# A mixture-of-experts kernel: the shared expert's gate and up as one-pass products of split operands, with most rows kept in HBM

## The chip, the cores and the metric

The kernel runs on one core of a Trainium2 chip. Its time is the device time of one execution, in microseconds (us). The trace comes from one profiled execution of the same program. Engines are named as in the profile: PE multiplies matrices, DVE and ACT do elementwise work, POOL and SP mostly issue DMAs; PEld is PE's loading of weights.

## The reference

The input x is [128, 64, 512]: 128 sequences of 64 steps with 512 features, all in float32. Two layers follow one another, each added to its input:

```python
x = x + ternary_ffn(gru(cond_2048, x))        # a scan over 64 steps
h = conv_causal(x, cond_2048) + b
x = x + moe(h) + shared(h)

# ternary_ffn: scale = mean(|W|); W3 = clip(round(W / scale), -1, 1) * scale; y = x @ W3.T + bias
# shared(h)  = silu(h @ sw_gate) * (h @ sw_up) @ sw_down       # 512 -> 704 -> 512, for all 8192 rows
# moe(h): softmax over 64 experts, the best 6 of them; each expert takes its first 64 rows,
#         silu(h @ w_gate) * (h @ w_up) @ w_down (512 -> 352 -> 512), weighted and summed
```

The sums of the 704 hidden features are what the change recomputes in another form; "gate" and "up" are the two products h @ sw_gate and h @ sw_up, "down" is the third.

## The kernel before

**Three stages.** The GRU goes through its 64 steps one after another (to about 1215 us). The causal convolution follows, as products with banded matrices (to about 1276 us). The last stage, to the end, holds router, shared expert and routed experts. It runs in iterations i = 0 to 15 of four steps each (NB = 4, so 512 rows). Iterations 0 to 7 are interleaved with the routing of all 16 blocks of rows, iterations 8 to 15 with the 64 routed experts, two at a time.

**Two ways to multiply float32.** A plain float32 product takes PE two instructions. A value can instead be split in two: the high part (`masked`, the low 12 bits cut off), and the rest. Three planes are then made, named h, l and s (the scaled mix of both), and a product becomes three one-pass products in type fp32r, hh, ll and ss, in two banks a and b, joined when the banks are emptied (`a * WHOLE + b`). The GRU is computed so, and the down product of iterations 1 to 7 (lines 1124 and 1137, planes `dparts` of the weights and `aparts` of the hidden values). A split costs DVE three operations and ACT one or two for each piece of 128 x 512 (lines 350, 1203, 1205).

**Seven products for eight.** The gate and up of all iterations go another way: `shared` treats the four steps and the four blocks of features as a 2 x 2 matrix of blocks and computes seven products of 256 columns in place of eight, in plain float32 (`winograd`, line 830, driven by class `Block`, lines 843 to 877). It needs sums and differences of the weights (`prepare_shared`, lines 790 to 793, tiles `st1`, `st2`, `st4`), made on DVE in iteration 0, and of the rows (the tile `space`). The 704 features are five chunks of 128 and a rest of 64, which line 1006 multiplies plainly. Iterations from 8 on use the same scheme for the down product too.

**Where rows are.** The convolution leaves its rows in two SBUF tiles, `hid0` and `hid1`, 32 steps each. All 64 steps are also stored to a table in HBM, `tab`, from which the routed experts gather (`put_rows`, line 1342), 40 of them issued on SP at 1281 us. `hid1`'s room becomes free when its rows are there; the planes of the down weights are put into it (`split_down`, line 1193 on). Blocks 8 to 15 come back from the table two at a time to be routed (`fetch_rows`, line 1374). After iteration 7 they come back as rows already turned, from a table `xts` (`load_xrows`, line 1431).

**Routing.** `route` turns a block's rows (line 1238), multiplies with the gate (1262), makes the softmax and picks six of 64 experts on DVE. It counts, in the tile `cum`, how many rows of each expert came up to each step. After iteration 7 `count_slots` makes the slots from this: a product psb (line 1515), then carry, `far` (1545), its absolute value on ACT (1555), a comparison (1556), and the products `found` (1572).

**What sets the order.** The code is written as generators: `for n, _ in enumerate(shared(i))` advances the shared expert by one group of products and takes pieces of `routing` and of `split_down` between. The order that is written is kept mostly; a scheduler may move an instruction ahead of others that do not need it, on the same engine, unless `tc.issue_after` ties it to another. Each engine then works its list strictly in order. Tiles in a pool wait for whoever used their room before.

**The steps of the GRU that matter here.** In step t, four transposes turn the state (`pst`, line 422), DVE and ACT split it into hh, hl and hs (lines 350, 356, 357, 436), and PE multiplies these with `whh` (line 339). In steps 2 and 3 DVE also converts the last of the GRU's weights (`convert`, lines 350, 367, 369), and step 3 has the sums for the ternary weights (`ternary`, line 463).

## Time and profile before

| what | value |
|---|---|
| median of 3 runs (lowest to highest) | 2431.18 us (2430.2 to 2432.18) |
| the profiled execution | 2432.05 us |
| its span, first to last instruction | 2430.1 us |
| granted clock of PE, mean | 0.999 |
| PE busy / PEld / DVE / ACT / POOL | 2416.7 / 1875.9 / 1588.1 / 502.7 / 447.7 us |
| DMA moved | 330.74 MB, 136 GB/s over the span |
| starts of iterations 0 to 8 (line 1006) | 1281.35, 1342.98, 1400.59, 1458.00, 1515.40, 1572.81, 1630.21, 1687.61, 1741.86 |

In the lines of the page and of the timelines, a group is named by its line, engine and operation, then output tile <- input tiles, the shape, and x followed by the number of instructions. In a timeline the first column is the start, the second the time from the start of the group's first instruction to the end of its last; in square brackets stands how long the engine was idle before it, and which instruction ended that. In a table by stretches each line has the stretch, its length, the busy time of PE, PEld, DVE, ACT and POOL, then the granted clock of PE, the mean share of the 16 DMA engines that was busy, and GB/s.

### The profile page before, as it was taken

The page shows a single profiled execution, that of the slowest core. Times are in us where ns is not written, and L with a number is a line of the kernel's source. Part 1 is how long each engine was busy: PE and PEld are TensorE (multiplying, and loading weights), DVE is VectorE, ACT ScalarE, POOL GpSimd, SP SyncE. Part 2 cuts the span into 40 slices and gives each one's busy share as a digit, 9 for nine tenths or more (in the row PEclk, how much of TensorE's full clock was granted, in tenths as well). Part 3 has the DMA queues.
Part 4 walks back from the last instruction along what each step waited for, and adds up shares of the span by engine and source line. Part 5 has one row for each costly group of instructions (what it writes and reads, how often), then busy time and mean ns, then how long its engine had stood idle before and what let it go on. Part 6 is the DMA issues. An engine that isn't in the chain of part 4 may idle for free.

```text
span 2430.1 us, 32183 instructions
## 1 busy us (share of the span) xinstructions
PE 2416.7 (99%) x12221; PEld 1875.9 (77%) x12221; DVE 1588.1 (65%) x3146; ACT 502.7 (21%) x920; POOL 447.7 (18%) x470
## 2 busy tenths in 40 slices
PE   9999999999999999999999999999999999999999
PEld 5788888888888888888896787888876666676667
DVE  8877777777777777777687767777753333343344
ACT  5211111111111111111123333333311111111111
POOL 1222221112112211221221000000012222222220
PEclk9999999999999999999999999999999999999999
DMA  5244443333222223222498223343459999899961
GB/s 189 76 85 85 81 77 63 61 68 67 58 56 61 58 53 58 60 57 44 110 344 299 42 43 72 102 114 91 143 147 291 290 297 308 265 320 312 281 176 40
DMA packets 469098, 330.74 MB, mean 136 GB/s; under 512 B 317136, under 2 KB 384720, under 8 KB 466768
## 3 DMA queue, kind: packets, MB, share of 16 engines
q1 hardware_dynamic: 439904, 254.47, 36.9%
q0 software_dynamic: 28896, 73.95, 13.4%
q8 instruction: 97, 1.59, 0.3%
q14 instruction: 57, 0.47, 0.1%
q10 hardware_dynamic: 144, 0.26, 0.0%
HBM read 241.83 MB, written 92.03 MB: 137 GB/s over the span
## 4 chain that ended last, share of the span: by engine, by line
PE 98%; DVE 1%; DMA 0%; ACT 0%; issue 0%; DVEq 0%; ACTq 0%
PE psa L339 9%; PE psw L339 9%; PE psx L339 9%; PE psz L830 7%; PE psw L830 7%; PE psx L830 7%; PE psb L339 5%; PE psz L339 5%; PE psy L339 5%; PE psf L339 5%; PE y L830 4%; PE py L1694 3%; PE pg L1668 3%; PE pu L1668 3%; PE y L1006 2%; PE psc L194 2%
## 5 line engine op out<-in xcount | busy, mean ns | idle before, releaser
L1678 DVE SCALAR_TENSOR_TENSOR a<-a,rw,pu 128x352 f32<-128x352 f32 x32 | 18.6, 580 | 213.0 <-PE pu L1668 198.8
L357 DVE SCALAR_TENSOR_TENSOR xs<-xl,xcut 128x512 fp32r<-128x512 f32 x63 | 103.6, 1644 | 65.6 <-POOL xl L356 65.6
L1214 POOL DMA_DIRECT2D out_dram<-hid x60 | 53.3, 1079 | 447.4 <-DVE hid L1150 368.0
L830 PE MATMUL psx<-hid,sw 128*128 128x256 f32 x512 | 132.3, 381 | 0.4 <-ACT g L870 0.4
L350 DVE TENSOR_SCALAR hcut<-pst 128x512 int32<-128x512 int32 x63 | 43.5, 691 | 130.1 <-PE pst L422 128.4
L491 ACT ACTIVATE rz<-rz 128x512 f32<-128x512 f32 x64 | 40.5, 633 | 335.8 <-DVE rz L490 334.8
L356 POOL TENSOR_TENSOR xl<-xp,xcut 128x512 fp32r<-128x512 f32 x60 | 83.1, 1386 | 145.7 <-PE psa L339 132.8
L830 PEld LDWEIGHTS psx<-hid,sw 128*128 128x128 f32 x512 | 94.3, 190 | 15.7 <-issue 2.9
L436 ACT CAST hh<-hcut 128x512 fp32r<-128x512 f32 x61 | 37.9, 621 | 325.0 <-DVE hcut L350 325.0
L272 POOL DMA_DIRECT2D q<-in_x_dram x36 | 19.3, 537 | 411.0 <-DMA out_dram<-q 331.1
L1694 PE MATMUL py<-wd,aeT 128*64 128x512 f32 (+1 forms) x288 | 88.6, 595 | 0.0
L830 PE MATMUL psw<-hid,st 128*128 128x256 f32 x320 | 83.0, 382 | 0.0
L1668 PE MATMUL pg<-wg,hid 128*64 128x352 f32 x384 | 81.1, 459 | 0.0
L1668 PE MATMUL pu<-wu,hid 128*64 128x352 f32 x384 | 81.1, 459 | 0.0
L1705 POOL DMA_INDIRECT out_dram<-hid,idxp x32 | 46.2, 1444 | 177.3 <-DMA out_dram<-hid,idxo 89.1
L1705 POOL DMA_INDIRECT out_dram<-hid,idxo x32 | 45.4, 1420 | 175.4 <-DMA out_dram<-hid,idxp 161.6
L870 ACT ACTIVATE g<-psx 128x256 f32<-128x256 f32 x80 | 30.7, 383 | 215.8 <-DVE aT L877 101.8
L504 ACT ACTIVATE n<-n 128x512 f32<-128x512 f32 x64 | 40.5, 633 | 166.7 <-DVE n L503 166.7
L339 PE MATMUL psa<-wih1h,xh 128*128 128x512 f32 x252 | 74.2, 415 | 0.0
L830 PE MATMUL y<-hid,st 128*128 128x256 f32 x280 | 74.0, 381 | 0.0
L272 POOL DMA_DIRECT2D xn<-in_x_dram x28 | 15.0, 536 | 318.4 <-DMA out_dram<-xn 271.1
L830 PE MATMUL psz<-hid,st 128*128 128x256 f32 x280 | 72.4, 380 | 0.0
(456 smaller groups left out, 6229.8 us busy)
## 6 DMA issues: line engine op xcount, KB each, us to landing
wg<-in_w_gate_dram SPq DMA_DIRECT2D x48, 704.0 KB
wu<-in_w_up_dram SPq DMA_DIRECT2D x48, 704.0 KB
wd<-in_w_down_dram SPq DMA_DIRECT2D x48, 512.0 KB
xc<-x1c SPq DMA_DIRECT2D x32, 512.0 KB
xp<-in_xT_dram POOLq DMA_DIRECT2D x62, 256.0 KB
out_dram<-hid POOLq DMA_DIRECT2D x60, 256.0 KB
tab<-hid SPq DMA_DIRECT2D x56, 256.0 KB
hid<-in_w_gate_dram SPq DMA_DIRECT2D x16, 704.0 KB
```

What stands on the lines that cost most here:

```text
L194: i = nc.tensor.matmul(ps[rows, j].rearrange("p h (u t) -> p h u t", u=2), xcs[sl % NCB][:, rows, g * 4 + j], tzs[sl % NCB][:, :, :, g * 4 ...
L339: i = nc.tensor.matmul(ps, lhs[:, k, :], rhs[:, k, :], start=start and k == 0, stop=stop and k == KD - 1, skip_group_check=True,)
L350: return nc.vector.tensor_scalar(dst.bitcast(I32), src.bitcast(I32), LOW, None, ALU.bitwise_and)
L356: i = engine.tensor_sub(lo, full, cut)
L357: nc.vector.scalar_tensor_tensor(mix, lo.bitcast(F32), -SPLIT, cut, ALU.mult, ALU.add)
L491: nc.scalar.activation(r, r, AF.Sigmoid)
L830: i = nc.tensor.matmul(ps.rearrange("p (j b) -> p j b", b=P) if len(r.shape) == 3 else ps, lhs(k), r, start=(first and k == 0), stop=(k == ...
L1006: nc.tensor.matmul(gu.rearrange("p (j b) -> p j b", b=P), swr[:, k].rearrange("p w n -> p (w n)"), rows[:, k], start=(k == 0), stop=(k == ...
L1214: nc.gpsimd.dma_start(out=out_t[t], in_=rows_of(i)[:, t % NB], accum_op=ALU.add)
L1668: nc.tensor.matmul(acc[halves[j]], self.xeT[:, k, halves[j]], self.ws[j][which][:, k, :], start=(k == 0), stop=(k == KD - 1),)
L1694: nc.tensor.matmul(py[halves[j]], self.aeT[:n, c, halves[j]], self.ws[j][2][:n, c, :], start=(c == 0), stop=(c == len(ech) - 1),)
L1705: nc.gpsimd.indirect_dma_start(out=out, out_offset=bass.IndirectOffsetOnAxis(ap=(idxp[:CAP] if j == 0 else idxo)[:, q : q + 1], axis=0), i ...
```

## The change

**Iterations 1 to 7** compute gate and up with split operands: for each chunk and for each of gate and up, three parts of four one-pass products of 512 columns (120 instructions in all). The weights' planes are `gparts` (g0 to g4, one for each chunk), the rows' planes `xparts`, made by `split_x(i + 1)` while the down products of iteration i run. ACT copies bank b, DVE joins both and multiplies. Iteration 0 computes gate and up as plain float32 products of 512 columns (`shared_plain`, 40 products). Iterations 8 to 15 are as before.

**Rows.** To make room, `hid0` keeps 12 steps (blocks 0 to 2), and `hid1` has the other 52. All 52 are stored in iteration 0 on SP, then their room becomes the planes g1 to g4, `dparts`, the scratch tiles `cut` and `xparts`. Every block from the fourth on is fetched from HBM for its iteration, into a ring of three areas in `hid0`; blocks are routed in a new order, as they are there, and 8 to 15 in between. The count in `cum` is started anew at step 32, and joined by one addition in `count_slots`.

**Weights.** In iteration 0 the shared weights are loaded ahead of the stores. After iteration 7 all pools are closed, the shared weights are loaded again (gate and up, 2.5 MB, and down, 1.28 MB), and `prepare_shared` runs there: chunk 0 between the iterations, 1 to 4 in iteration 8. `split_down` moves to iteration 1 and loads its pieces again.

**GRU.** In step 3 the products `psb <- wih1s, xs` come behind the transposes; the second half of the conversion in step 2 comes behind hs of that step; the sums for the ternary weights come behind the cell of step 3.

```diff
 def shared_split(i):                       # new, iterations 1 to 7
+    gu = rest_product(rows_by_k(i))
+    masters = [ring[:, c % 3] for c in range(full)]
...
+    for c in range(full):
+        for which in range(2):
...
+            for n, ps in ((2, b), (0, a), (1, a)):
+                for k in range(KD):
+                    m = nc.tensor.matmul(
+                        ps,
+                        gparts[c][n][:, which, k],
+                        xparts[n][:, k],
+                        start=n != 1 and k == 0,
+                        stop=n != 0 and k == KD - 1,
...
+                if n == 2:
+                    nc.scalar.copy(v, b)
...
+            nc.vector.scalar_tensor_tensor(v, a, WHOLE, v, ALU.mult, ALU.add)
+            if which == 0:
+                nc.scalar.activation(g, g, AF.Silu)
+                if c == 0:
+                    rest_split(sg, gu, aTr)
+            else:
+                mul(v, v, g)
+            next(split, None)
+            yield
...
+        split = split_block(masters[c], c)
+    downs.append([*split][-1])
+    yield from down_split(i)

+def split_x(i):
+    rows = rows_by_k(i)
+    for k in range(KD):
...
+        masked(cut, rows[:, k])
+        nc.scalar.copy(xh, cut)
+        nc.vector.tensor_sub(xl, rows[:, k], cut)
+        nc.vector.scalar_tensor_tensor(
+            xs, xl.bitcast(F32), -SPLIT, cut, ALU.mult, ALU.add
+        )
+        yield

 if i == 0:
+    for n in range(NEAR, NI):
+        put_rows(n)
     later.close()
...
+    work = (
+        w
+        for ws in (split_gate_up(0), split_x(1), *map(split_gate_up, range(1, full)))
+        for w in ws
+    )
 if i == 1:
...
+    work = split_down()

 def count_slots():
+    nc.vector.tensor_tensor(
+        cum[:, TH:],
+        cum[:, TH:],
+        cum[:, TH - 1 : TH].to_broadcast([P, TH, NE]),
+        ALU.add,
+    )

+w1 = ctx.enter_context(tc.tile_pool(name="w1", **right))      # after iteration 7
...
+load_xrows(HALF)
+load_sw(w1)
+load_swd()
...
+prepare_shared(0)

-            products(b, xs, ws, start=True, stop=c == 2)         # GRU, step 3
+            with tc.issue_after(turns[-1].ins) if (t, c) == (3, 1) else nullcontext():
+                products(b, xs, ws, start=True, stop=c == 2)
...
+                        convert(raw_h[c], whh[c], cuts, range(KD // 2))
+                        with tc.issue_after(mixes[-1].ins):
+                            convert(raw_h[c], whh[c], cuts, range(KD // 2, KD))
```

## Prediction

> **What bounds the kernel now.** I read the busy table and the chain's shares first, to learn which engine a saved microsecond must come from.
>
> ```profile
> PE 2416.7 (99%) x12221; PEld 1875.9 (77%) x12221; DVE 1588.1 (65%) x3146; ACT 502.7 (21%) x920; POOL 447.7 (18%) x470
> ...
> PE 98%; DVE 1%; DMA 0%; ACT 0%; issue 0%; DVEq 0%; ACTq 0%
> ```
>
> PE is idle for 13.4 us of the 2430.1 us span, so the time is PE's work plus very little. Any PE work saved counts in full, any wait that the change puts in front of PE counts in full too, and there are no gaps in which a new wait could hide. Second, the table by stretches, for the stage that is changed:
>
> ```profile
> 1400.00:1500.00 100.00, 100.00 (x505) 80.41 (x504) 74.17 (x206) 36.06 (x70) 5.20 (x6) 1.00 0.25 57
> 1305.00:1310.00 5.00, 5.00 (x29) 4.39 (x28) 4.01 (x11) 0.60 (x2) 0.00 (x0) 1.00 1.04 396
> ```
>
> In a hundred microseconds of iterations 2 and 3, PE is busy for 100.0, DVE for 74 (fourth value), ACT for 36, and the granted clock is 1.00. Between 1305 and 1310 the DMA engines are full (share 1.04, 396 GB/s): those are the rows going to HBM. Third, PE's timeline, for the price of one product in each form:
>
> ```profile
> 1560.98 1.07 PE L1124 MATMUL psw<-dl,al 128*128 128x512 f32 x4
> 1561.89 1.07 PE L1124 MATMUL psz<-ds,as 128*128 128x512 f32 x4
> ...
> 1576.56 1.03 PE L830 MATMUL psx<-hid,sw0first 128*128 128x256 f32 x4
> 1577.43 1.03 PE L830 MATMUL y<-hid,st 128*128 128x256 f32 x4
> ...
> 1324.05 7.89 PE L1099 MATMUL y<-swd,aT 128*128 128x512 f32 x18
> 1331.87 1.13 PE L1109 MATMUL y<-swdr,aTr 64*128 64x512 f32 x4
> ```
>
> I take start to start. Four one-pass instructions of 512 columns take 0.907 us, 0.2268 each. A 7-product block's product of 256 columns is two instructions (x4 is two products): 0.865 / 2 = 0.4325. Plain fp32 of 512 columns: 18 instructions in 7.82 us, two to a product, 0.868.
>
> **Iterations 2 to 6: -15.3 us.** The old gate and up are 5 chunks x 7 products x 2 halves = 70 products x 0.4325 = 30.27 us. The new are 5 chunks x 2 x 3 parts x 4 = 120 x 0.2268 = 27.22. That is -3.05 for each iteration, if DVE and ACT keep up. In that phase PE also has the rest product (8 instructions, 3.5 us) and the routing of two blocks (32 transposes at 0.109 and logits of 3.6 us with the small ones: 7.5 us, 3.7 a block), so 38.2 us; DVE has for each chunk two evictions and a product (3 x 0.60) and a split (0.34 + 0.60 + 0.60), 16.7 us in all, and two routing blocks at some 5.9, together 28.4. It fits, with a quarter to spare. Behind the last chunk, DVE has 4 evictions (2.4 us) and the next rows' split (4 x 1.54 = 6.2) beside 15.4 us of down products (68 x 0.2268). So I expect 57.41 (iterations 2 to 6 start 57.4 apart) to become 54.36; bounds -10 (a microsecond of new waits in each) and -17. The fetches back are four DMAs of 256 KB, 2.6 us at 396 GB/s, and are issued over 8 us ahead of their transposes; were that cover gone, a block would cost up to 2.6 us. Iteration 7 routes two blocks now and had one: 54.36 against 54.25, +0.1.
>
> **Iterations 0 and 1: +6.5 us.** Iteration 0 goes to plain fp32: 40 x 0.868 = 34.7 against 30.27, of which some 1.6 us come back, because the present one waits (psx at 1290.88 has 0.43 of idle) for differences of the weights that are no longer made: +2.5 or so, so it ends at 1281.35 + 61.63 + 2.5 = 1345.5. Iteration 1 with one routing block would be 54.36 - 3.7 = 50.6 and end at 1396.1, 4.5 us ahead of 1400.59. But its planes and split rows lie in the room of the later rows, which must be in HBM first:
>
> ```profile
> 1281.41 32.37 SPq L1342 DMA_DIRECT2D tab<-hid  x40
> ...
> 1316.96 0.52 POOL L1367 MEMSET dr<- 64x512 f32 x1 [36.67 <-DMA tab<-sc]
> ```
>
> The room was free at 1316.96. Now 12 more rows of 256 KB go through it (12 x 0.66 = 8 us), and some 2.3 MB of weight loads stand in front of them on SP's queue (5.8 us): about 1331. From there DVE has, in this order, the first weights' planes (2 pieces), the rows (4) and the other planes (8), all ahead of the first evictions of iteration 1. One piece I take from the conversions of the down weights:
>
> ```profile
> 1326.85 0.42 DVE L350 TENSOR_SCALAR cut<-swd 128x512 int32<-128x512 int32 x1
> 1327.31 0.69 DVE L1203 TENSOR_TENSOR cut<-swd,cut 128x512 f32<-128x512 f32 x1
> 1327.91 0.42 DVE L1291 TENSOR_TENSOR sc<-pst,nmax 128x256 f32<-128x256 f32 x1
> 1328.25 0.68 DVE L1205 SCALAR_TENSOR_TENSOR ds<-cut 128x512 fp32r<-128x512 f32 x1
> 1329.04 0.43 DVE L350 TENSOR_SCALAR cut<-swd 128x512 int32<-128x512 int32 x1
> ```
>
> 2.19 us from piece to piece, 0.34 of it other work; the two buffers and ACT's copies set this pace, since three operations alone are 1.54. Fourteen pieces at 1.85 are 26 us, and iteration 0's evictions and routing beside them some 4: 1361. PE can do the rest product (3.5) and chunk 0 (5.4) from 1345.5, to 1354.4, and then has no bank: 6.6 us of stall. Some 2.7 come before it (the first planes and rows are ready at 1331 + 6 x 1.85 + 4 = 1346 and are read from 1349 on only if no evictions stand between, which they do), and the six pieces of the down weights, also in iteration 1, some 1.7 us later: 11 us. So -4.5 + 11 = +6.5. Bounds: -4.5 if the pieces go at 1.54 and the room is free by 1320; +11 if they take 2.19.
>
> The rate is the step's weakest term. *The Trainium skill, "DMA: Bandwidth & Descriptors", Where 436 GB/s comes from, holds about 358 GB/s to be the limit of HBM for a core, and speaks against this change; the row at 1305 shows 396 with one core running. By the page, 8 + 5.8 us would be 15.3, the room free 1.5 us later and the sum 1.5 us worse, an estimate; I go by the row.*
>
> **The hand-over from iteration 7 to 8: +7.2 us.** The built order of PE puts the count's product psb and the first 28 `found` products ahead of iteration 8's rest product; before, this product and the 256-column ones stood there and covered the chain:
>
> ```profile
> 1741.86 3.60 PE L1006 MATMUL y<-hid,swr 128*128 128x512 f32 x8
> 1745.30 0.19 PE L1515 MATMUL psb<-nrow,before 128*128 128x64 bf16 x1
> ...
> 1749.82 1.07 PE L1572 MATMUL found<-pos,hid 128*64 128x67 bf16 x14
> ```
>
> Let T0 be the end of the last down product (1741.86 here). On DVE the last eviction and four small operations come first; nrow stood at T0 + 1.2 (1743.02). Then psb, and from psb to `found` 4.5 us (1745.30 to 1749.82): carry, two far (1.04 each), Abs on ACT (0.95), is_lt (1.0). Now four differences for iteration 8's weights (4 x 0.34) stand between, so `found` is at T0 + 7.2 and, with 28 products in 2.0 us, the rest product at T0 + 9.2. The 28 were paid before, so +7.2. Bounds: +4 (psb to `found` without the differences, less what DVE gains) and +9 (the four casts of the mask on ACT, 3.89 us, in the way). Iteration 8 also makes four chunks' differences that iteration 0 made before (16 x 0.34 = 5.4 us of DVE, beside 57 us of PE) and waits for the reloaded down weights (1.28 MB, 3.3 us, issued at T0, needed after the gate): +1, bounds 0 and +4. The add to the later counts is one operation of 2048 elements, about four of 512 (2.4 us), hidden behind 6.4 us of down products; without that cover it costs 2.4. From iteration 9 on the order is as before.
>
> **Steps 2 and 3: -3.1 us.**
>
> ```profile
> 72.75 0.60 PE L422 MATMUL pst<-ident,h 128*128 128x128 f32 x4
> 76.10 1.36 PE L339 MATMUL psx<-whh0h,hh 128*128 128x512 f32 x4 [2.75 <-ACT hh L436]
> 77.25 1.91 PE L339 MATMUL psw<-whh2h,hh 128*128 128x512 f32 x4
> ```
>
> From the transposes' end (72.75 + 0.44) to psx 2.91 us pass, and the next three groups of four take 1.15, 1.71 and 1.58 in place of 0.91: 1.7 more. Four products (0.91) move into the gap, and the conversions that hold DVE at 73 to 76 move behind hs. The bare way from transposes to hh, by step 4 (0.44 + 0.7 + 0.6, with latencies some 2.3), leaves 1.4 or 1.5 of it. 4.6 - 1.5 = 3.1; bounds -4.4, and 0 if the conversions moved make the next step's first use late. The reductions behind step 3's cell have a whole step of 17 us.
>
> *The Trainium skill, "VectorE: DVE Perf Modes", The TRN2 errata, gives an fp32 operation of 512 elements as (512 + 151) / 0.96 = 691 ns, 0.69 in the row at 1327.31; but the next operation starts 0.60 after that, so the fixed part overlaps. By the page's figure the 42 operations of the 14 pieces would take up to 3 us longer, an estimate, and the sum would be nearer to nought.*
>
> **Sum.** -15.3 + 0.1 + 6.5 + 7.2 + 1 - 3.1 = -3.6 against the profiled execution's 2432.05: 2428.4. The runs' median, 2431.18, lies 0.87 below it: 2427.5, which I round to 2427. So most of what the one-pass products save is given back at two places, where planes are made and where the count begins.
>
> **Rivals.** (1) *The saving arrives.* The pieces of iteration 1 go at 1.54 and the hand-over costs its lower end: -4.4 - 15.3 - 4.5 + 4 = -20, 2411; half of that is 2417 to 2420. For it: DVE is 25% idle now; against it: the row of 2.19, and the order, in which evictions stand behind eight pieces. (2) *Slower: iteration 1 is bound by DVE from late rows.* Each microsecond by which the last row lands after 1331 is one of PE's, as is each 0.07 us that a piece takes above 1.85. From +8.5 us on (1339.5, or 2.45 a piece) the change is over 0.2% slower; at both upper ends with the hand-over at +9, it is 2431.2 + 5 = 2436 to 2440. For it: DMA is full to 1316 already. (3) *It doesn't do what it says*: banks are not emptied in time, and iterations 2 to 6 stay at 57.4. Then +11.7, 2443. For it: DVE's 28.4 of 38.2 us in one phase; against it: a regular order in which nothing waits for a later chunk.
>
> **How the numbers follow.** What a measurement can tell from no change is about 0.2%, 4.9 us: faster is below 2426.3, slower above 2436.0. Forecast 0.50 (own range 2421 to 2433; 0.2 of it below the line, 0.3 within), rival 1 0.26, rival 2 0.16, rival 3 0.08. Faster 0.46, within 0.30, slower 0.24. The range runs from rival 1's end to rival 2's, 2411 to 2440, and leaves out rival 3 and tails.
>
> **What would show it.** Iterations 2 to 6 starting 54.4 apart: the products are right. Iteration 2's start near 1404 (1407 less the 3.1 of steps 2 and 3): the planes; 1393 would be rival 1, 1412 rival 2. An idle PE of some 7 us ahead of `found`: the hand-over. psx 1.4 behind its four moved products in step 3: the reordering. Wrong above all would be a DVE that runs pieces and evictions side by side better than two buffers let the old conversions run.

## The result and the profile after

The changed kernel is slower by a third of a per cent: 2440.18 us in the median against 2432.25 for the kernel before on the same chip, a ratio of 1.0032 with a 95% interval of 1.002 to 1.0044. I had said 2427, and 2411 to 2440. The profiled execution took 2439.71 us, its span is 2438.0, the granted clock 0.996 (0.999 before). From its page, the busy times and the chain's shares by engine:

```profile
PE 2409.3 (99%) x12021; PEld 1839.5 (75%) x12021; DVE 1596.9 (66%) x3059; ACT 550.2 (23%) x958; POOL 447.7 (18%) x470
...
PE 96%; DVE 2%; issue 1%; ACT 0%; DMA 0%; DVEq 0%; ACTq 0%
```

PE's busy time fell by 7.4 us and the span grew by 7.9: PE was idle for 13.4 us and is now for 28.7, and DVE holds 2% of the chain. The busy time hides one thing more: products that run at half the clock count as busy.

The starts of the iterations (rest product; iteration 8 behind `found`) and T0, the end of iteration 7's last down product, give a ledger that adds up to the span's +7.9:

| step | before, us | after, us | measured | predicted |
|---|---|---|---|---|
| to iteration 0 (steps 2, 3) | 1281.35 | 1278.21 | -3.1 | -3.1 |
| iteration 0 | 61.63 | 64.53 | +2.9 | +2.5 |
| iteration 1 | 57.61 | 67.27 | +9.7 | +4.0 |
| iterations 2 to 6 | 287.02 | 273.26 | -13.8 | -15.3 |
| iteration 7, to T0 | 54.25 | 56.56 | +2.3 | +0.1 |
| T0 to iteration 9 | 57.17 | 67.03 | +9.9 | +8.2 |
| rest, iteration 9 on | 631.07 | 631.14 | +0.1 | 0 |

**Iterations 2 to 6** go as worked out. The table by stretches, for the hundred microseconds of iterations 2 and 3:

```profile
1415.00:1515.00 100.00, 100.00 (x496) 77.97 (x495) 80.44 (x194) 46.66 (x78) 5.19 (x6) 1.00 0.29 77
```

PE has no idle time and the full clock; DVE went from 74 to 80. They start 54.65 apart; 54.36 was the forecast, 57.4 the time before.

**Iteration 1.** PE's timeline, with the idle time and what ended it in brackets:

```profile
1361.91 2.00 PE L1183 MATMUL psx<-xh,g2h 128*128 128x512 f32 x4 [3.08 <-DVE g L1199]
1363.71 1.89 PE L1183 MATMUL y<-xs,g1s 128*128 128x512 f32 x4
1365.41 1.11 PE L1183 MATMUL psx<-xl,g2l 128*128 128x512 f32 x4
...
1394.09 0.80 PE L1053 MATMUL y<-dh,ah 128*128 128x512 f32 x1 [4.00 <-ACT ah L1303]
1394.69 1.91 PE L1053 MATMUL y<-dl,al 128*128 128x512 f32 x4
```

Four one-pass products take 1.07 here as a group elsewhere; behind the waits of 3.08 and 4.00 they take 2.00, 1.89 and 1.91. The stretches give the reason in the column behind POOL, the clock:

```profile
1360.00:1365.00 5.00, 3.09 (x8) 2.42 (x9) 4.94 (x23) 3.36 (x7) 0.52 (x1) 0.70 0.34 107
...
1390.00:1395.00 5.00, 1.00 (x3) 0.81 (x3) 5.00 (x16) 2.94 (x5) 0.00 (x0) 0.77 0.11 26
1395.00:1400.00 5.00, 5.00 (x14) 3.85 (x14) 5.00 (x19) 1.14 (x2) 0.00 (x0) 0.54 0.00 0
```

Between 1395 and 1400 PE is busy all the time and does 14 instructions, where 22 of these products have room at 0.2268 us each; DVE is busy for every microsecond. The waits of iteration 1 are 0.84, 0.65, 3.08, 1.27 and 4.00 us, 9.84 in all. The slow products cost 1.7 (8 of them in 3.50 us from 1361.91, for 1.81) and 2.7 (16 in 6.32 from 1394.09, for 3.63). Where the clock is at half can be laid out by stretches:

```profile
1362.02:1365.43 3.41, 3.41 (x9) 2.64 (x10) 3.32 (x18) 2.44 (x5) 0.00 (x0) 0.50 0.49 156
1392.74:1399.57 6.83, 5.48 (x13) 4.32 (x14) 6.83 (x26) 2.33 (x5) 0.00 (x0) 0.50 0.00 0
```

It is 0.50 for 3.41 us and for twice as long, and 1.00 in the 27.31 us between them. Half of PE's busy time in the two stretches, 1.7 and 2.7 us, is just what the products lost.

**The hand-over**, PE's timeline:

```profile
1741.64 0.19 PE L1709 MATMUL psb<-nrow,before 128*128 128x64 bf16 x1 [1.66 <-DVE nrow L1707]
1747.28 2.07 PE L1769 MATMUL found<-pos,high 128*64 128x67 bf16 x28 [5.44 <-DVE high L1753]
1749.27 4.61 PE L1088 MATMUL y<-high,swr 128*128 128x512 f32 x8
```

`found` comes 7.45 us behind T0 (1739.83), the rest product 9.44; 7.2 and 9.2 were forecast. The rest product takes 4.61 where it took 3.60 before: half clock again, behind 5.44 of idle.

### The profile page after: what moved, and what is told of

Read it like the earlier page. It is cut to its first block, busy times and chain, and to the rows that moved or that the text cites. A ratio compares the mean times of both kernels' runs of the same rounds, so it can differ in the third digit from the quotient of the medians.

```text
span 2438.0 us, 31786 instructions
## 1 busy us (share of the span) xinstructions
PE 2409.3 (99%) x12021; PEld 1839.5 (75%) x12021; DVE 1596.9 (66%) x3059; ACT 550.2 (23%) x958; POOL 447.7 (18%) x470
## 4 chain that ended last, share of the span: by engine, by line
PE 96%; DVE 2%; issue 1%; ACT 0%; DMA 0%; DVEq 0%; ACTq 0%
PE psa L340 9%; PE psw L340 9%; PE psx L340 9%; PE psb L340 5%; PE psz L340 5%; PE psy L340 5%; PE psf L340 5%; PE psw L863 4%; PE psx L863 4%; PE psz L863 4%; PE py L1891 3%; PE pg L1865 3%; PE pu L1865 3%; PE psx L1183 3%; PE psz L1183 3%; PE psc L195 2%
## 5 line engine op out<-in xcount | busy, mean ns | idle before, releaser
L1865 PE MATMUL pg<-wg,low 128*64 128x352 f32 x384 | 81.1, 459 | 0.0
L1865 PE MATMUL pu<-wu,low 128*64 128x352 f32 x384 | 81.1, 459 | 0.0
L1902 POOL DMA_INDIRECT out_dram<-high,idxo x32 | 45.7, 1427 | 177.5 <-DMA out_dram<-high,idxp 165.7
L1902 POOL DMA_INDIRECT out_dram<-high,idxp x32 | 45.9, 1434 | 168.0 <-DMA out_dram<-high,idxo 86.7
L340 PE MATMUL psy<-wih0s,xs 128*128 128x512 f32 x252 | 68.2, 392 | 0.5 <-DVE rz L499 0.5
L340 PE MATMUL psb<-wih1s,xs 128*128 128x512 f32 x252 | 68.4, 392 | 0.0
L340 PE MATMUL psa<-wih1l,xl 128*128 128x512 f32 x252 | 68.2, 392 | 0.0
L340 PE MATMUL psw<-wih2l,xl 128*128 128x512 f32 x252 | 68.1, 391 | 0.0
L340 PE MATMUL psx<-wih0l,xl 128*128 128x512 f32 x252 | 67.9, 391 | 0.0
L340 PE MATMUL psw<-wih2h,xh 128*128 128x512 f32 x252 | 67.9, 391 | 0.0
```

Of the source, the lines that this page charges most:

```text
L340: i = nc.tensor.matmul(ps, lhs[:, k, :], rhs[:, k, :], start=start and k == 0, stop=stop and k == KD - 1, skip_group_check=True,)
L1865: nc.tensor.matmul(acc[halves[j]], self.xeT[:, k, halves[j]], self.ws[j][which][:, k, :], start=(k == 0), stop=(k == KD - 1),)
L1902: nc.gpsimd.indirect_dma_start(out=out, out_offset=bass.IndirectOffsetOnAxis(ap=(idxp[:CAP] if j == 0 else idxo)[:, q : q + 1], axis=0), i ...
```

## The experiments

Two theories stood after this. One: the waits cost more than their length, because of the clock. The other: it is the order of the work that makes the waits, so that moving work gives them back. Later a third came for the hand-over: DVE has too much to do there, in whatever order.

### The clock: warm_fill, gap_ladder, gap_short

*warm_fill* puts 12, 16 and 7 products without use into the three long waits (`filler(m, 12)` behind a product of chunk 2, `filler(mm[1, 2, full - 3], 16)` in the first down products, 7 behind psb).

> The changed kernel with idle PE kept busy: products whose result nobody reads stand in its three longest waits (12 one-pass products ahead of psx<-xh,g2h in iteration 1, 16 ahead of the last y<-dh,ah there, 7 plain ones between psb and found); every other instruction is in the order of the changed kernel. The extra products add work and no value. Theory of the clock: what follows a wait of over 3 us runs at half the clock for some microseconds (1.75 us lost at 1361.9 to 1366.4, 2.7 at 1394.1 to 1400.2, 0.9 in iteration 8's rest product), and this work keeps the clock at 1.0: about 5 us less, 2435, with iteration 1 at 62.5 to 63.5 us in place of 67.3 and the rest product of iteration 8 back at 3.5 us. Rival: the products after the waits are slow because their operands come late from DVE and ACT; then the filled waits change nothing, 2440, and any extra work that ends too late makes it slower.

Measured: 2437.06 us, 1.0021 of before (1.0012 to 1.003), 3.1 less than the changed kernel. The stretch of the first wait in this kernel:

```profile
1355.00:1370.00 15.00, 13.74 (x60) 10.59 (x61) 14.83 (x46) 11.05 (x20) 0.52 (x1) 1.00 0.15 44
```

The clock is 1.00, iteration 1 takes 64.54 us for 67.27, the rest product of iteration 8 3.70 for 4.61. Part of what the clock gave back turns into waits again (0.72 us at 1365.95, 1.00 at 1754.82): of 5.3 us of slow products 3.1 come back. Shown: the clock is a cost of its own. A later run, count_behind, shows it by chance a second time. It has the same wait at the same place, but there the clock stays at 1.00, and the four products behind it take 1.19 us for 2.00:

```profile
1361.96 1.19 PE L1183 MATMUL psx<-xh,g2h 128*128 128x512 f32 x4 [3.06 <-DVE g L1199]
```


*gap_ladder* asks how the cost depends on the wait. It is the kernel before, with a chain of 1, 3, 6, 10 and 15 small subtractions on POOL that one product waits for, ahead of the rest product of iterations 2 to 6.

```diff
+    GAPS = {2: 1, 3: 3, 4: 6, 5: 10, 6: 15}
...
+        nc.scalar.copy(gap, ps[:, 0, 0])
+        for _ in range(n):
+            nc.gpsimd.tensor_sub(gap, gap, ident)
...
+            gates.append(nc.tensor.matmul(ps[:, 0, 1], ident, gap, start=True, stop=True))
```

> The kernel before with a made wait of PE ahead of the rest product of iterations 2 to 6: a small product, a copy on ACT, then 1, 3, 6, 10 and 15 operations of 128x128 on POOL, and a product that reads the last; all of the iteration's other products are tied behind it. The values that it makes are not used. Estimated idle time of PE: about 2, 3, 4, 6 and 8 us. Theory of the clock: short waits (up to 2 or 3 us) cost their own length alone; those of some 4 us and more are followed by a stretch at half the clock, so that the 8 instructions of the rest product take 4.4 to 7 us in place of 3.5 and the cost is the wait plus 1 to 3.5 us. Rival: the rest product takes 3.5 us behind every one of them, and the slow products in the changed kernel had late operands.

*gap_short* makes shorter ones in the same places.

> The kernel before with five short made waits of PE ahead of the rest product of iterations 2 to 6 (a copy on ACT of 16, 64 and 128 columns, then the same with one operation on POOL of 16 and 64 columns), estimated idle time 1.8 to 2.9 us; the values are not used. The waits of 3.2 to 10.6 us were each followed by some 3 to 5 us at half the clock, 1.6 to 2.4 us lost, and one of 2.75 us in the GRU of the kernel before by a mean clock of 0.66. Theory: below some 2 us nothing happens, and from there on it depends on when the wait falls: some of the five have the rest product at 3.5 us, the longest ones do not. Rival: the clock falls behind every wait, however short, in proportion.

gap_ladder took 2476.87 us, gap_short 2442.46 (one run each). PE's timeline of gap_ladder, gates and rest products:

```profile
1403.96 0.49 PE L809 MATMUL lg<-gap,ident 128*128 128x128 f32 x2 [3.03 <-POOL gap L807]
1404.29 5.29 PE L1022 MATMUL y<-hid,swr 128*128 128x512 f32 x8
...
1672.15 0.79 PE L809 MATMUL lg<-gap,ident 128*128 128x128 f32 x2 [10.44 <-POOL gap L807]
1672.74 6.03 PE L1022 MATMUL y<-hid,swr 128*128 128x512 f32 x8
```

and of gap_short:

```profile
1518.67 0.49 PE L810 MATMUL lg<-gap,ident 128*128 128x128 f32 x2 [0.62 <-ACT gap L805]
1518.99 3.60 PE L1024 MATMUL y<-hid,swr 128*128 128x512 f32 x8
...
1638.58 0.43 PE L810 MATMUL lg<-gap,ident 128*128 128x64 f32 x2 [2.92 <-POOL gap L807]
1638.86 5.35 PE L1024 MATMUL y<-hid,swr 128*128 128x512 f32 x8
```

The five waits of gap_short came out as 0.62 (three times), 0.99 and 2.92 us, mostly shorter than meant. After 0.62 and 0.99 us the eight products take 3.60 to 3.68, after 2.92 us they take 5.35; after the 3.03, 4.06, 5.66, 7.78 and 10.44 us of gap_ladder they take 5.29, 5.83, 5.18, 5.48 and 6.03. That is 1.5 to 2.4 more, and it does not grow in step with the wait. The theory of gap_ladder had the limit too high: it let waits of up to 2 or 3 us go free, and its shortest, 3.03, paid in full. Between 0.99 and 2.92 us these two runs have no wait. Of the 44.8 us by which gap_ladder exceeds the kernel before, the waits are 31.0 and the slow products 9.8; the other 4.0 stand at the added chain around them and were not taken apart.

### One part alone: gru_alone, iter1_plain

*gru_alone* is the kernel before with the reordering of steps 2 and 3 only.

> The kernel before with the reordering of steps 2 and 3 of the GRU alone. Prediction's step: -3.1 us, 2432.2 to 2429.1, with psx 1.4 us behind the four moved products. Rival: the gain at step 3 is given back at step 4, whose operands the moved conversions and sums make late: 2432.

Measured: 2429.22 us, 0.9986 of before (0.9977 to 0.9996), by the medians 3.6 us; iteration 0 starts 2.65 earlier. That term holds alone. Part of it is the clock: PE's wait in step 3 is 1.12 us here for 2.75 before, and from 76 to 79 us the clock is 1.00 for 0.66.

*iter1_plain* is the changed kernel with iteration 1 in plain fp32 too, so that all planes of weights and rows are made during iteration 1, for iteration 2, and the down weights are split from the tile that is there.

```diff
+            if i == 1:
...
-                    for ws in (split_gate_up(0), split_x(1), *map(split_gate_up, range(1, full)))
+                    for ws in (*map(split_gate_up, range(full)), split_down(), split_x(2))
...
-            if i == 1:
+            if i == 2:
...
-                work = split_down()
...
-            for n, _ in enumerate(shared_split(i) if i else shared_plain(i)):
+            for n, _ in enumerate(shared_split(i) if i > 1 else shared_plain(i)):
```

> The changed kernel with iteration 1 as plain float32 too (gate, up and down as in iteration 0), so that all planes (ten pieces of gate and up, six of down, four of rows) are made on DVE during iteration 1, for iteration 2. PE does more work: with one routing block iteration 1 is about 64.5 - 3.4 = 61.1 us, against 67.3 now. Theory (the planes of iteration 1 stand ahead of its evictions on DVE, 9.8 us of idle PE and 4.4 of half clock): 2440.2 - 6 = 2434, no idle over 1 us and a clock of 1.0 in iterations 1 and 2. Rival: the stall comes from the rows that land late, whatever needs the planes: then DVE is stuck behind them as long as before, and iteration 1 stays at 65 or more: 2438 to 2441.

Measured: 2435.11 us, 1.0011 (1.0002 to 1.002). Iteration 1 takes 61.77 us in place of 67.27 though its gate and up alone cost 7.5 us more (34.7 for 27.2), and PE is idle in it for 0.03 us. Shown: the pieces on DVE, with the clock behind their waits, are what iteration 1 lost.

### The hand-over: does the order cost it?

*count_behind* puts psb and `found` behind the shared expert's products, as they lay before.

```diff
-            nc.tensor.matmul(ps_b, before, nrow, start=True, stop=True)
+            with behind(products):
+                nc.tensor.matmul(ps_b, before, nrow, start=True, stop=True)
```

> The changed kernel, with the count's product psb and the found products tied behind the rest product and the first 256-column products of iteration 8 (order alone, nothing left out). Theory: the hand-over costs PE 7.3 us of idle time (1.66 ahead of psb, 5.44 ahead of found, and 0.2) and another 0.9 because the rest product after it runs at a granted clock of about 0.5 (8 instructions in 4.45 us, 3.5 elsewhere). So about 2440.2 - 8 = 2432, iteration 8's rest product within 0.3 us of the last down product, and a clock of 0.99 or more from 1735 to 1760. Rival: the wait only moves, since far, its absolute value and the comparison now stand behind other work of iteration 8 on DVE and the products of iteration 8 wait for them: 2436 or more, with new idle time of 4 us or more in iteration 8.

Measured: 2442.22 us, 1.0044 (1.0031 to 1.0058): slower still. The rest product starts at T0, but then PE waits 2.48 us at 1752.02 (for ACT's u, line 892) and 2.78 at 1765.69 (for DVE's aT, line 909), both followed by half clock (6.83 and 3.41 us of it); from T0 to iteration 9 it is 68.63 us. The theory that only the order costs something fell here.

*pool_diff* makes the differences of the weights on POOL, *pool_behind* has the count behind the products as well, *pool_behind_plain1* iteration 1 plain besides (`nc.vector.tensor_sub` becomes `nc.gpsimd.tensor_sub` at lines 824 to 827).

> The changed kernel with the weight differences of iteration 8 (20 operations of 128x256, 0.34 us apart on DVE, 6.8 us) made on POOL in place of DVE; the order of PE is left, psb and found ahead of the rest product. Theory now: the hand-over and iteration 8 together (67.0 us from the last down product to the start of iteration 9, 57.2 before) are bound by DVE, whose work is the count, these differences and the down weights' sums. Without the 4 of the first chunk between far and the comparison, found comes 1.4 us earlier (T0 + 6.1), and iteration 8 loses its waits of some 1 us: 2440.2 to about 2437.5, the 67.0 to 64.5. Rival (the wait is the chain of the count alone, whatever else DVE does): found no earlier than T0 + 7.1, 2440.

> The same differences on POOL, and psb and found behind iteration 8's first products, as in the run that moved the wait (68.6 us from the last down product to iteration 9). Theory (DVE bound): with 6.8 us of DVE taken away the 7 us of waits in iteration 8 go, since the count now lies beside products and DVE has room: 58 to 61 us in place of 67.0, so 2440.2 - 7 = 2433, down to 2431. Rival (the count's chain and the down weights' sums alone fill DVE, or POOL's slower operations come too late for the st products): 64 us or more, 2437 or more.

> Both repairs together: iteration 1 plain, with the planes made during it (2435.1 alone), and the differences on POOL with the count behind iteration 8's first products. Theory: the two waits that the change added are independent, so the savings add: 2435.1 - 7 = 2428, below the kernel before (2432.9), of which 3.1 come from the GRU and the rest from iterations 2 to 6. If the repair at iteration 8 fails, 2433 to 2435.

Measured: 2443.15 (1.0042, 1.0027 to 1.0058), 2442.54 (1.004, 1.0024 to 1.0055) and 2437.67 us (1.0022, 1.0013 to 1.0031): no gain from any of them; all three are at or past what was expected for a repair that fails. POOL's timeline in pool_diff:

```profile
1744.21 1.45 POOL L825 TENSOR_TENSOR st<-sw1first,st 128x256 f32<-128x256 f32 x1
1745.63 1.57 POOL L826 TENSOR_TENSOR sw1first<-sw1first 128x256 f32<-128x256 f32 x1
...
1750.91 0.72 POOL L825 TENSOR_TENSOR st<-sw,st 128x256 f32<-128x256 f32 x1
```

One difference takes 0.72 to 1.57 us on POOL in these lines, for 0.34 from start to start on DVE; and DVE gets slower beside it. Its timeline in pool_behind:

```profile
1746.87 0.69 DVE L924 TENSOR_TENSOR space<-swd 128x512 f32<-128x512 f32 x1 [1.04 <-DMA swd<-in_sw_down_dram]
1747.48 0.75 DVE L1717 SCALAR_TENSOR_TENSOR shift<-carry,nrow 128x64 f32<-128x64 bf16 x1
1748.15 1.23 DVE L925 TENSOR_TENSOR space<-swd,space 128x512 f32<-128x512 f32 x1
1749.30 1.21 DVE L926 TENSOR_TENSOR swd<-swd 128x512 f32<-128x512 f32 x1
```

The first sum takes 0.69, the next 1.23 and 1.21; in count_behind, with no subtraction on POOL, they take 0.68. What DVE was relieved of it lost again: in pool_diff `found` comes 7.2 us behind T0 for 7.45, where 6.1 was expected, in pool_behind PE waits 2.77 us at 1752.83 for DVE's `u` (line 894), and T0 to iteration 9 is 70.1 us.

*early_diff* makes all five chunks' differences on DVE ahead of the last evictions of iteration 7 and all the sums of the down weights in the third chunk; *early_diff_behind* adds the count behind the products, *early_diff_behind_plain1* the plain iteration 1.

```diff
-    prepare_shared(0)
+    with tc.issue_after(evicted[1]):
+        for c in range(EARLY):
+            made = prepare_shared(c)
```

> The changed kernel with all 20 weight differences on DVE ahead of iteration 7's last two evictions, where DVE is idle for 6.8 us (1733.2 to 1740.0), and the down weights' sums moved from ahead of iteration 8's first products to its third chunk; psb and found are still ahead of the rest product. Theory (iteration 8 is bound by DVE): found about 1.3 us earlier (T0 + 6.1, then bound by the mask's casts on ACT), and no more waits in iteration 8: from the last down product to iteration 9 67.0 to 63 or 64, 2440.2 to 2437. Rival (loads land too late): the differences wait for the reloaded weights and hold up the evictions behind them, psb comes later than T0 + 2.5, no gain or a loss.

> The same, and psb and found tied behind iteration 8's first products, as in the run that moved the wait. Theory (DVE bound): what filled DVE between 1740 and 1770 there was the differences (6.8 us) and the down weights' sums (2.7) beside the count; with both out of the way the count lies beside products, as in the kernel before: 57.2 to 60 us from the last down product to iteration 9, against 67.0 in the changed kernel and 68.6 in that run, so 2440.2 - 8 = 2432. Rival (the count itself cannot be covered): 64 or more, 2437 or more.

> The same with iteration 1 plain and the planes made in it (2435.1 alone, 5.1 less than the changed kernel). Theory: 2435.1 - 8 = 2427, faster than the kernel before by 5 us, and than the GRU's part alone (2429.2) by 2. If the hand-over is not mended: 2434 or more.

Measured: 2447.57, 2452.04 and 2446.66 us (1.0064, 1.0083 and 1.0061). All three fail for a reason of their own. PE's timeline of early_diff_behind:

```profile
1757.44 5.25 PE L1091 MATMUL y<-high,swr 128*128 128x512 f32 x8 [18.05 <-DMA high<-xts]
```

SP is one queue in order. The rows of iteration 8 were issued on it at 1727.46 in the changed kernel; here their load came to stand behind others and was issued at 1742.95, and PE waited 18 us for it (5.2 in early_diff, whose count comes first, and 18 in the third). So these runs say nothing on the theory that DVE has too much to do; a version with the rows' load kept in its place wasn't tried.

### The hand-over: is it DVE's sum of work?

*no_diff* and *no_diff_behind* leave the 20 differences out, in the changed kernel and in count_behind.

```diff
-        if n in sums_:
-            return sums_[n][:, :, c * P : (c + 1) * P]
+        n = {4: 3, 6: 2, 5: 1}.get(n, n) if n in sums_ else n
...
-    prepare_shared(0)
```

> The changed kernel, in which iterations 8 to 15 use plain weight blocks where they need sums and differences of blocks, so that the 20 small DVE operations (4 ahead of the count, 16 in iteration 8) are left out (the output then means nothing from iteration 8 on; the number and shapes of PE's products are the same). Theory (DVE sets the pace from the end of iteration 7 to the end of iteration 8): found comes 4 x 0.34 = 1.4 us earlier, at about 6.1 behind the last down product, the wait ahead of it stays above 3 us with its half clock, and iteration 8 loses 0.5 to 1.5 us more: from the last down product to iteration 9 67.0 becomes 64.5, the time 2437.7. Rival (only the half clock and the hand-over's chain cost something, the differences inside iteration 8 are covered): 65.7 and 2438.8.

> As no_diff, with the count's products (psb, found) placed behind those of the shared expert, as in count_behind. Theory (count_behind failed since DVE had differences, down-weight sums and count all at once): the new waits of 2.5 and 2.8 us and their half clock go, and from the last down product to iteration 9 it is 59 to 60 us in place of 68.6: the time 2433. Rival (the wait comes from the order or from late weights, not from DVE's load): 66 or more, the time 2439.5 or above.

Measured: 2439.95 us (1.0031, 1.0019 to 1.0043), which is past even the rival's 2438.8, and 2438.11 (1.002, 1.0011 to 1.003), between the two and nearer to the rival. Without the cover the differences are worth next to nothing (66.9 us from T0 to iteration 9 for 67.03); with it they are worth 2.8 (65.80 for 68.63), a third of what I expected. DVE's timeline of no_diff_behind showed what else stood there:

```profile
1744.45 0.22 DVE L1707 TENSOR_SCALAR carry<-psb 128x64 bf16<-128x64 f32 x1
1746.79 0.69 DVE L923 TENSOR_TENSOR space<-swd 128x512 f32<-128x512 f32 x1 [2.12 <-DMA swd<-in_sw_down_dram]
1747.40 0.22 DVE L1711 SCALAR_TENSOR_TENSOR shift<-carry,nrow 128x64 f32<-128x64 bf16 x1
```

DVE waits 2.12 us for the reloaded down weights, and the count's `shift`, which needs nothing of them, is queued behind.

*down_later* (count_behind, with `prepare_down` in the third chunk) and *down_later_plain1* (with the plain iteration 1) take only that away, and keep all work:

```diff
-        if i == NI // 2:
-            prepare_down()
...
+                if n == 7 and i == NI // 2 and c == 2:
+                    with tc.issue_after(cur.summed.ins):
+                        prepare_down()
```

> count_behind with all work kept, but the four sums of the down weights (4 x 0.6 us of DVE) are made in the third chunk of iteration 8 and not at its start. Theory: the wait of 2.48 us near 1752 and its half clock (1.6 or so) go, the later one of 2.8 near 1766 stays or moves: from the last down product to iteration 9 64 to 65 us, the time 2438. Rival (these sums are not what is late): as count_behind, 68.6 and 2442.

> down_later with iteration 1 in plain fp32 as well, as in iter1_plain (all work kept): 5 us less than down_later by what iter1_plain gained. Theory: 2433. If it is under 2429.2 it beats the steps 2 and 3 alone and the kernel before. Rival: 2437, as the sum of iter1_plain and an unimproved hand-over.

Measured: 2440.74 (1.0034, 1.0021 to 1.0047) and 2436.06 us (1.0015, 1.0005 to 1.0025). The wait near 1752 did shrink to 0.46, but one of 2.93 came at 1763.99: 67.76 us from T0 to iteration 9. The rivals were nearer in both.

*no_sums_behind* takes the differences, the sums and the wait away together; *count_spread* (down_later_plain1, in which the count advances at `n % 6 == 1` and not at `n % 4 == 1`) takes nothing away but asks less of DVE at a time.

> no_diff_behind, in which the four sums of the down weights are left out too (iterations 8 to 15 use plain blocks of them; the output means nothing from iteration 8 on, PE's products are the same in number and shape). In no_diff_behind DVE waited 2.12 us at 1746.8 for the reloaded down weights, with the count's chain queued behind, and spent 2.4 on the sums. Theory (what DVE has to do and to wait for behind iteration 7 sets the hand-over): of the 65.8 us from the last down product to iteration 9, 4.5 and the half clock behind the waits go; 59 to 61 and 2432. Rival (the order of PE is to blame): 65 or more, 2437.5.

> down_later_plain1 (all work kept), in which the count's groups come every six groups of products of iteration 8 and not every four. Theory (DVE falls behind because the count's 4.1 us a group, the evictions and the differences come at more than 4.4 us of work in 4.4): it falls behind by 1.2 us a group in place of 1.9, the wait of 2.93 near 1758 shrinks to 1 or less, from the last down product to iteration 9 64 us in place of 67.7: 2432.5. Rival (a delay at the start of the iteration that nothing gives back): 67, 2435.5.

Measured: 2431.52 us (0.9996, 0.9986 to 1.0006), as the theory had it, and 2434.01 (1.0007, 0.9997 to 1.0016), halfway between theory and rival. In count_spread the wait that was to shrink from 2.93 us to 1 or less is 2.87, with half clock behind it; it lies 4 us earlier, and from T0 to iteration 9 it is 66.08 us for the 67.7 of down_later_plain1. So a gain of 1.6 us there is measured, and the reason that I gave for it is not shown. From T0 to iteration 9 no_sums_behind takes 58.62 us, and its only wait of PE there is this:

```profile
1759.71 1.13 PE L862 MATMUL psz<-high,sw 128*128 128x256 f32 x4 [0.66 <-DVE aT L908]
```

The stretch of 25 us behind T0, in the kernel before, count_behind and no_sums_behind:

```profile
1740.00:1765.00 25.00, 25.00 (x142) 18.50 (x140) 21.57 (x55) 12.19 (x19) 1.70 (x2) 1.00 0.95 292
```

```profile
1740.00:1765.00 25.00, 19.50 (x85) 12.57 (x83) 24.04 (x58) 9.45 (x13) 1.71 (x2) 0.86 0.89 281
```

```profile
1740.00:1765.00 25.00, 24.34 (x135) 17.41 (x135) 24.20 (x60) 11.84 (x19) 1.70 (x2) 1.00 0.87 269
```

DVE is as busy in the last two (24.04 and 24.20); PE gets 85 instructions done in the one and 135 in the other, at a clock of 0.86 and 1.00. The busy share of DVE does not tell the two apart; what stands in its list ahead of what PE waits for does. From T0 to iteration 9:

| kernel | us | what it does to DVE there |
|---|---|---|
| before | 57.17 | |
| after | 67.03 | 11 us more, count ahead |
| count_behind | 68.63 | 11 us more, count behind |
| no_diff_behind | 65.80 | 6.8 less than that |
| down_later | 67.76 | 2.4 us moved later, wait gone |
| count_spread | 66.08 | as down_later, count slower |
| no_sums_behind | 58.62 | 9.2 less, wait gone |

The steps do not add up: against count_behind, leaving the differences out gives 2.8 us, moving the sums with their wait 0.9, leaving out both 10.0. How much of the 10.0 is work and how much the wait for the reloaded weights is not shown.

The 11 us are three sums of rows more (3 x 0.60), four of the down weights (4 x 0.60) and 20 differences (20 x 0.34). Where the sums were in the kernel before, DVE's timeline shows:

```profile
1729.32 0.68 DVE L999 TENSOR_TENSOR hid<-hid 128x512 f32<-128x512 f32 x1
1729.92 0.68 DVE L892 TENSOR_TENSOR space<-swd 128x512 f32<-128x512 f32 x1
1730.52 0.68 DVE L1000 TENSOR_TENSOR hid<-hid 128x512 f32<-128x512 f32 x1
...
1732.93 0.68 DVE L1054 TENSOR_TENSOR hid<-hid 128x512 f32<-128x512 f32 x1
```

There they lay beside the last down products of iteration 7, 8 to 12 us ahead of T0; and the differences were made in iteration 0. In the changed kernel rows and weights come back from HBM, and all of it is behind T0.

**A version that beats both kernels** is gru_alone, at 2429.22 us. Of the versions that keep the one-pass products, the best are count_spread (2434.01) and iter1_plain (2435.11); none beat the kernel before.

## Why the prediction was wrong, point by point

- **Right: what bounds the kernel, and the price of the products.** Each wait put in front of PE counted in full. Iterations 2 to 6 gained 13.8 for 15.3: 54.65 us each for 54.36.
- **Right: steps 2 and 3.** -3.14 for -3.1, and gru_alone gives it without the rest (2.65 at iteration 0, 3.6 in the medians). PE's timeline has psx 1.30 us behind the place where a fifth moved product would have begun (the bracket, 1.13, counts from the modelled end of the fourth); I had said 1.4 or 1.5:

```profile
72.39 1.17 PE L340 MATMUL psb<-wih1s,xs 128*128 128x512 f32 x4
74.69 1.21 PE L340 MATMUL psx<-whh0h,hh 128*128 128x512 f32 x4 [1.13 <-ACT hh L447]
```

- **The step that failed first: the sum of iterations 0 and 1** ("So -4.5 + 11 = +6.5"), which measured +12.6, over its upper bound of +11. The mechanism, planes that DVE makes late, was right (iter1_plain). The 11 us of stall came as 9.84, but that the length fits is in part luck: I had 9.3 around chunk 0 and 1.7 for the pieces of the down weights; measured are 4.57 up to 1361.91 and 5.27 among the down products, which wait for the planes `as` and `ah` of the hidden values. What the sum put at nothing, without a reason, is the half clock behind a wait: 4.4 us in iteration 1, shown by warm_fill and gap_ladder. With the 0.9 at the hand-over it is 5.3 of the 11.5 us between the -3.6 that I forecast and the +7.9 of the span. With the waits as measured and the clock the sum is -4.5 + 9.8 + 4.4 = 9.7. Of the 2.8 us that are left, 0.4 are iteration 0's (2.9 for 2.5; its own figures, 34.7 - 30.27 - 1.6, give 2.85), 0.6 its split logits (below, iteration 7) and 0.3 the products as in iterations 2 to 6; 1.5 were not taken apart. The trace of before had it in view. The table by stretches, 73 to 82 us:

```profile
73.00:76.00 3.00, 0.35 (x4) 0.11 (x1) 3.00 (x6) 2.61 (x5) 2.15 (x3) 1.00 0.34 107
76.00:79.00 3.00, 2.90 (x9) 2.28 (x10) 1.83 (x4) 0.04 (x1) 1.07 (x2) 0.66 0.93 318
79.00:82.00 3.00, 3.00 (x12) 2.41 (x11) 1.26 (x3) 0.00 (x0) 0.00 (x0) 0.77 1.08 338
```

Behind the wait of 2.75 at 76.10 the clock is 0.66 and 0.77. I had counted the three slow groups there ("1.7 more") in the gain of steps 2 and 3, without asking why they were slow: 1.7 is what the wait of 3.08 us then cost in iteration 1. *The Trainium skill, "TensorE: Matmul & The Clock Gate", What's actually happening, has the array at half clock after an idle window of about 3.4 us, and back at the full one after as long of activity, the window running freely. The runs agree on the half clock, and its stretches of 3.41 us and twice that fit such a window; on the wait that brings it they differ, 2.75 us was enough in the kernel before and 3.06 was not in count_behind.*
- **The rows' room was free when I said, and the planes were late all the same.** At 374 to 407 GB/s between 1280 and 1325 (one stretch had 353), the stores were done and the first piece began at 1328.12; my 1331, less the 3.1 us of steps 2 and 3, is 1327.9. *The Trainium skill, "DMA: Bandwidth & Descriptors", Where 436 GB/s comes from, whose 358 GB/s I had weighed and set aside, would have been the worse guide here.* But the second piece came 6 us behind the first. DVE's timeline, then ACT's:

```profile
1328.12 0.43 DVE L351 TENSOR_SCALAR cut<-sw0first 128x512 int32<-128x512 int32 x1 [1.13 <-DMA tab<-sc]
...
1334.40 0.43 DVE L351 TENSOR_SCALAR cut<-sw1first 128x512 int32<-128x512 int32 x1 [4.19 <-ACT g0h L1324]
```

```profile
1332.78 1.07 ACT L1038 COPY hid<-y 128x512 f32<-128x512 f32 x2 [5.78 <-PE y L1036]
1333.74 0.63 ACT L1324 CAST g0h<-cut 128x512 fp32r<-128x512 f32 x1
```

The piece's copy g0h was queued on ACT behind the evictions of iteration 0, which waited 5.78 us for PE. I had counted what stands in front of the pieces on SP and DVE, and not on ACT. The fourteenth piece ended at 1362.45, 34.3 us behind the first's start, where I had 26 + 4. From 1340 to 1380 DVE is then busy for 4.89 or more of every five microseconds.
- **Iteration 7, "+0.1", measured +2.3.** Of this 1.3 us are its logits: 32 products, which take 5.17 us here and 3.90 in iteration 6. In iteration 7 the scheduler put one product of the shared expert between the first two and the other 14, twice. PE's timeline of iteration 7, and the 16 in one group in iteration 6:

```profile
1698.23 0.65 PE L1403 MATMUL lg<-hid,gw 128*64 128x256 f32 x2
1698.80 0.50 PE L1183 MATMUL psz<-xl,g1l 128*128 128x512 f32 x1
1699.24 1.94 PE L1403 MATMUL lg<-hid,gw 128*64 128x256 f32 x14
```

```profile
1665.08 1.95 PE L1403 MATMUL lg<-hid,gw 128*64 128x256 f32 x16
```

Sixteen take 1.95 together and 2 + 14 take 2.59. At 0.12 us each, where a product of 128 columns with the same 256 elements takes 0.22, two logits seem to run at once, and a lone one between others not; this is read from the lines and no run tried it. PE is idle for 0.27 of the 2.2 us; the rest is not settled.
- **The hand-over, "+7.2" and "+1", measured +9.9.** The chain to `found` was right to 0.25 us. Some 0.9 more is the rest product at half clock, the same term that iteration 1 lacked; the rest of iteration 8, where PE is idle for 0.73 us only, is some 0.5 longer than the "+1". So in the changed kernel the two terms were nearly right. What was wrong behind them, and does not show in the sum, is "5.4 us of DVE, beside 57 us of PE": in the first 25 us DVE, busy there for 21.57 already in the kernel before, had no such room. In that trace it is busy for 4.92 and 5.00 of the five-microsecond stretches from 1750 to 1760, and the only share of DVE that I had read, 74 of 100, was that of iterations 2 and 3. The sums of rows and down weights that came from under iteration 7's down products I had not counted at all. count_behind showed that with the cover for the count restored the loss is as large; no_sums_behind that it goes when DVE's added work and its wait for the reloaded weights go. The two causes stand in for each other: as long as the count is ahead, PE waits for it and DVE works its list off; when it is behind, PE runs and waits for DVE later.
- **The rivals.** Rival 2 is what came by its sign and its place, iteration 1 bound by DVE, and by half of its mechanism: the rows were not late, the pieces were (34.3 us for 30). Its "from +8.5 us on" was not reached by the waits, 9.84 for 11, but by the clock, 4.4. Rival 3 did not come.

## What to carry to other kernels

A wait of PE of about 3 us or more can cost more than its length: here all but one of the waits from 2.75 us on had half clock around or behind them, for 0.9 to 2.7 us on top, not in step with the length. Look for groups that take twice their time behind an idle bracket, and put the clock into the sum of every wait that a change makes. Room on an engine is read in the stretch where the work will lie, not from its share of the span or of another stage; and when data comes from HBM that used to lie in SBUF, list everything that was computed from it early, since all of that moves behind the load. A repair of one cause that gives nothing back may only have uncovered the next one: take the suspects away together before dropping them.

## What the runs showed of the hardware that I had not expected

- What the half clock costs doesn't follow the length of the wait: 1.5 to 2.4 us lost on eight plain products after waits of 2.92 to 10.44 us, nothing after 0.62 and 0.99 us; products without use in the wait keep the clock at 1.00 (warm_fill).
- The length of one wait doesn't say whether the half clock comes. It did not come behind 3.06 us in count_behind, nor behind 1.78 and 1.55 in pool_diff, whose stretch from 1755 to 1770 has a clock of 1.00. It did come in no_diff_behind, from 1752.73 to 1756.14 behind waits of 1.44 and 1.11 close together, and from 1766.38 to 1769.79 behind one of 1.86.
- In the changed kernel the half clock lasted 3.41 us once and 6.83 twice (1362.02, 1392.74 and 1744.32, each at 0.50), and half of the time in which PE worked plain or one-pass products in it was lost.
- POOL and DVE slowed each other: a 128x256 subtraction took POOL 0.72 to 1.58 us, and DVE's 128x512 ones beside it took 1.21 and 1.23 for 0.69 (pool_diff, pool_behind).
- One product of the shared expert among sixteen of the 64-column logits made these 0.64 us longer (2.59 for 1.95).
